# A recurrent kernel of 128 steps: biases loaded as single rows and spread by products with ones, x of steps 2 and 3 loaded later, sums and turns of the first steps rearranged

## The chip, the cores and the metric

The kernel runs on one core of one Trainium2 chip. The metric is device time in microseconds (us) from launch to end. Before the change the median of three runs is 1335.53 us (1335.13 to 1337.05).

## The reference

A gated recurrent unit runs over x (64 sequences, 128 steps, width 512) from the state h0 = cond_1024 (64 x 512), and its output is added to x. All is float32. Cut to what matters:

```python
def step(h, inp):
    x_t, prop = inp
    comb = jnp.concatenate([x_t, h], axis=-1)
    z = jax.nn.sigmoid(comb @ Wz + bz)
    r = jax.nn.sigmoid(comb @ Wr + br)
    comb2 = jnp.concatenate([x_t, r * h], axis=-1)
    h_cand = jnp.tanh(comb2 @ Wh + bh)
    h_new = (1.0 - z) * h + z * h_cand
    h_next = jnp.where(prop, jnp.tanh(h_new @ Wp + bp), h_new)
    return (h_next, h_new)
# prop holds at every fourth step but the last; the result is x + all h_new
```

Wz, Wr, Wh are 1024 x 512: the upper 512 rows meet x_t, the lower 512 meet the state. Wp is 512 x 512; bz, br, bh, bp have 512 elements.

## The kernel before

**Tiling.** The 64 sequences and two halves (S = 2) of the 512 columns together fill the 128 partitions: partition s*64 + b holds sequence b and columns s*256 to s*256 + 255. N = 256, C = 2 blocks of 128 columns each. A product (`product`, `products`, L191 to L205) multiplies one of four pieces of 128 rows of a weight with a turned left side, one matmul per half s into its 64 partitions. The weights over x are in `wx`, those over the state in `wh[0..2]` (R, Z, H in this order) and `wp`.

**The order of the work** is written out by hand, one queue for each engine; the schedule is manual, and each engine works its instructions in the order of the program. A step t (loop at L674) goes: products of the state with wh R (L723), sigmoid (L740), r*h; products with wh Z (L751), meanwhile the turns of r*h (L755), sigmoid twice for z and 1 - z (L764, L765), `keep` = (1-z)*h (L766); products of the turned r*h with wh H (L796), tanh (L802), two operations of VectorE that make h (L803, L808), and the turn of h for the next step (L820, L822). Every fourth step has the products with Wp as well. GpSimd adds h to x in place (L901).

**Filling.** What depends on x alone is put between these products as units out of a queue: `fill(n)` (L417) issues the next n units; the last unit of a batch leaves a function that empties its PSUM tiles, which `read_out()` (L424) issues later. PLACES and TAIL (L637 to L645) say how many units go where. The results, with the biases, are gathered in `cp`; `seed(i, t)` (L409) copies them into the PSUM tile of gate i (`rc`, `zp`), so that the products of the state are added on top.

**Two ways to the x products.** Steps 0 to 3 use `plain(t)` (L428): 12 units of plain products into scratch tiles (`scratch_q`, `_r`, `_a`, `_x`); plain(0) and (2) use q and r, plain(1) and (3) use a and x. From step 4 on, four steps are taken together and their products are made with fewer multiplications out of sums of x and sums of weights, twice nested. Sums of the weights: `sum_outer` (into `tw`, VectorE, L318), `sum_inner(i, eng)` (three operations into `tt`, L328) and `sum_inner_1(i, eng)` (one in place, L333), on VectorE or GpSimd as called. Sums of x: `sum_raw12`, `sum_raw34`, `sum_raw4`, `sum_s12`, `sum_s34` on GpSimd. A batch of them is made by `batch` (L509); before the change, batches of the first group of four steps (g = 1) write scratch q, r, x in this order after a, later ones r, x, q (L557). `pair_left` and `pair_right` (L623, L629) add the results of group 1 on GpSimd with the biases.

**Turning.** `turn` (L212) transposes one block of 128 columns by 4 matmuls against the identity (recorded as L219) into the PSUM tile `turn_0` or `turn_1`, and one copy (L210) takes it out. `turn_x(t, eng)` (L243) turns x of steps 0 to 7 in this way, with ScalarE copying where no engine is named. Later x is turned by a transposing DMA (`words_x`, `planes_x`, `join_x`).

**The head.** Before the steps (L72 to L153) the loads are issued: SyncE's queue holds the first half of x of steps 0, 1, then the weights in the order of use; ScalarE's queue holds the other half of that x and half of wx R. GpSimd waits at L130 (`held`) until x has landed, and then issues h0 and six loads of 64 KB that spread the rows of br, bz, bh over 64 partitions each (`load_bias`, L119). x of steps 2, 3 stands on SyncE's queue between wh R and wh Z (L138). TensorE meanwhile runs products of zeros (`idle(n)`, L179), turns x of steps 0 and 1, and does plain(0) and plain(1) with the turn of h0 in between (L657 to L669).

Of the kernel before, what the change touches and what calls it, by code (L numbers as in the profile page):

```python
# [9 lines left out]
F32 = mybir.dt.float32  # L10
BF16 = mybir.dt.bfloat16
# [6 lines left out]
def kernel(  # L18
# [29 lines left out]
    nc = tc.nc  # L48
    B, T, D = x.shape
    H = h0.shape[1]  # L50
    P = 128
# [19 lines left out]

    zeros = one.tile([P, 2 * N], BF16, tag="cq", name="zeros")  # L72
    nc.vector.memset(zeros, 0.0)
    ident = const.tile([P, P], F32, name="ident")
    make_identity(nc, ident)
    ones = const.tile([1, B], F32, name="ones")
    nc.gpsimd.memset(ones, 1.0)
    ident16 = const.tile([P, P], BF16, name="ident16")
    nc.vector.tensor_copy(ident16, ident)


    wx = const.tile([P, K, 3, H], F32, name="wx")
# [3 lines left out]
    tw = {n: const.tile([P, S, S, 3, P], F32, name=f"tw_{n}") for n in (2, 3, 4)}  # L86
    tt = const.tile([P, 7, 3, S, 3, P // 2], F32, name="tt")
    gates_in = (Wr, Wz, Wh)
    def load_x(tile_, t0, n, j=0):
        for s in range(S):  # L90
            nc.sync.dma_start(
                out=tile_[s * B : (s + 1) * B, j : j + n, :], in_=x[:, t0 : t0 + n, ts(s, N)]
            )
# [25 lines left out]
    def load_bias(i, eng):  # L119
        for s in range(S):  # L120
            eng.dma_start(
                out=bias_in[s * B : (s + 1) * B, i, :],
                in_=(br, bz, bh, bp)[i][ts(s, N)]
                .rearrange("(o n) -> o n", o=1)
                .broadcast_to([B, N]),
            )


    held = const.tile([1, 1], F32, name="held")
    nc.gpsimd.tensor_copy(held, xr[0][0:1, 0, 0:1])  # L130
    for s in range(S):
        nc.gpsimd.dma_start(out=h_init[s * B : (s + 1) * B, :], in_=h0[:, ts(s, N)])
    for i in (R, Z, H_):
        load_bias(i, nc.gpsimd)
    for i in range(3):
        for k in (0, 2):
            load_w(wh[i], gates_in[i][D:, :], k, k + 2, nc.sync)
        if i == 0:  # L138
            load_x(xr[0], 2, 2, 2)

    dummy = const.tile([1, 1], F32, name="dummy")
# [29 lines left out]

    def cut(ps):
        return ps.rearrange("p (c n) -> p c n", c=C)

    bias0 = bias[:, 0, 0:3, :]
    bias_d = const.tile([P, 3, P], F32, name="bias_d")
# [2 lines left out]
    def idle(n):  # L179
        for i in range(n):  # L180
            s = i % S
            nc.tensor.matmul(
                (rc, zp)[i // S % 2][s * B : (s + 1) * B, :, :],
                lhsT=zeros[:, :B],
                rhs=zeros,
                start=True,
                stop=True,
            )
# [14 lines left out]
    def product(ps, lT, w, k, start=False):  # L203
        s0, c0 = divmod(k, C)
        products(ps, lT[:, c0, ts(s0, B)], lambda s: w[:, k, ts(s, N)], start)  # L205
# [24 lines left out]
    def new_T(tag, name):  # L230
        return two.tile([P, C, P], F32, tag=tag, name=name)
# [11 lines left out]
    def turn_x(t, eng=nc.scalar):  # L243
        g, i = divmod(t, Q4)
        new_xT(g)
        src = xr[g] if g < 2 else early[g]
        for c in range(C):
            turn(src[:, i, :], xT[g][:, i], c, f"xT_{t}", eng)
# [79 lines left out]
    def sum_inner(i, eng):  # L328
        eng.tensor_sub(tt[:, i - 1, 1], inner(i, 1, 1), inner(i, 0, 1))
        eng.tensor_add(tt[:, i - 1, 0], tt[:, i - 1, 1], inner(i, 0, 0))  # L330
        eng.tensor_sub(tt[:, i - 1, 2], inner(i, 1, 0), tt[:, i - 1, 0])
# [31 lines left out]
    def sum_s12(g):  # L363
        v = xT[g]
        o = sx[g, "o12"] = one.tile([P, 2, 2, P], F32, tag="o12", name=f"o12_{g}")
        nc.gpsimd.tensor_add(o[:, 0], v[:, 2:4, 0, :], v[:, 2:4, 1, :])
        nc.gpsimd.tensor_sub(o[:, 1], o[:, 0], v[:, 0:2, 0, :])
        s = sx[g, 56] = one.tile([P, 4, 2, B], F32, tag="s56", name=f"s56_{g}")
        four([s[:, n] for n in range(4)], o[:, :, 0], o[:, :, 1])
# [139 lines left out]
    def batch(n, ms):  # L509

        def region(ps, m):
            return ps[:, m].rearrange("p g u -> p (g u)")

        def unit(ps, m, j, e, start):
            g, i = ms[m]
            a, b = terms(i)[e]
            products(
                region(ps, m),
                lhs(g, a, j),
                lambda s: factor(b, j)[:, s],  # L520
                start and m == 0 and e == 0,
            )

        def units(ps, j, start):
            return [
                lambda m=m, e=e: unit(ps, m, j, e, start)
                for m, (_, i) in enumerate(ms)
                for e in range(len(terms(i)))
            ]

        def blocks():
            return MB[n].rearrange("p m b g (a u) -> p m b a g u", a=2)

        def end_1():
            MB[n] = mbp.tile([P, 2, 2, 3, P], F32, tag="mb", name=f"mb_{ms[0][0]}_{ms[0][1]}")
            for m, (g, i) in enumerate(ms):
                M[g, i] = MB[n][:, m]
            nm = len(ms)
            T2[n] = one.tile([P, 2, 3, P // 2], F32, tag="cx", name=f"cx_{ms[0][0]}_{ms[0][1]}")
            q1 = one.tile([P, 2, 3, P // 2], F32, tag="cq", name=f"cq_{ms[0][0]}_{ms[0][1]}")  # L540
            nc.scalar.copy(T2[n][:, :nm], x_ps[:, :nm])  # L541
            nc.scalar.copy(q1[:, :nm], q_ps[:, :nm])
            nc.vector.tensor_add(T2[n][:, :nm], r_ps[:, :nm], T2[n][:, :nm])  # L543
            nc.vector.tensor_add(blocks()[:, :nm, 0, 0], a_ps[:, :nm], q1[:, :nm])

        def end_2():
            q2 = one.tile([P, 2, 3, P // 2], F32, tag="cq", name=f"cq2_{ms[0][0]}_{ms[0][1]}")
            nm = len(ms)
            nc.scalar.copy(q2[:, :nm], q_ps[:, :nm])  # L549
            nc.vector.tensor_add(blocks()[:, :nm, 0, 1], r_ps[:, :nm], q2[:, :nm])  # L550
            nc.vector.tensor_add(blocks()[:, :nm, 1, 0], x_ps[:, :nm], q2[:, :nm])
            nc.vector.tensor_add(blocks()[:, :nm, 1, 1], q_ps[:, :nm], T2[n][:, :nm])  # L552

        free = units(a_ps, 2, True)
        one_ = [units(r_ps, 5, True), units(x_ps, 7, True), units(q_ps, 1, True)]

        one_ = sum(one_ if ms[0][0] >= FIRST else one_[2:] + one_[:2], [])  # L557
        two_ = units(x_ps, 4, False) + units(q_ps, 6, False) + units(r_ps, 3, False)
        seq = [(u, None) for u in free + one_ + two_]
        size = sum(len(terms(i)) for _, i in ms)  # L560
        for n_units, end in ((4 * size, end_1), (7 * size, end_2)):
            seq[n_units - 1] = (seq[n_units - 1][0], end)
        return seq
# [59 lines left out]
    def pair_left(a, p1, p2):  # L623
        nc.gpsimd.tensor_add(
            M[1, p2], M[1, p2], bias0.unsqueeze(1).to_broadcast([P, 2, 3, P])
        )
        add(c_block(1, a, 0), m_(1, p1), m_(1, p2))
# [17 lines left out]
    )  # L645


    idle(24)
    turn_x(0, nc.vector)
    idle(8)  # L650
    turn_x(1, nc.vector)
    idle(12)
    nc.gpsimd.tensor_sub(bias_d, bias[:, 1, 0:3, :], bias0)
    h = h_init
    hT = new_T("hT", "hT_init")
# [18 lines left out]
    for t in range(T):  # L674
# [48 lines left out]
        for k in ORDER:  # L723
            product(slots[R], hT, wh[R], k)
        if t < 2:
            turn_x((2, 6)[t])
        if t == 1:
            for i in (7, 4):
                sum_inner(i, nc.gpsimd)
                sum_inner_1(i, nc.gpsimd)  # L730
        read_out()
        if t == 2:
            pair_left(0, 1, 2)
        if u == 0 and pair >= 1 and odd - 2 < LAST:
            outer_u2(odd - 2)
        if t == 3:
            sum_s12(FIRST)
        rh = two.tile([P, N], F32, tag="rh", name=f"rh_{t}")
        for c in range(C):
            nc.scalar.activation(act_ps[c], slots[R][:, ts(c, P)], AF.Sigmoid)  # L740
# [9 lines left out]

        for k in ORDER[: 2 if thin else 3]:  # L751
            product(slots[Z], hT, wh[Z], k)
        rhT = new_T("rhT", f"rhT_{t}")
        for c in range(C):
            turn(rh, rhT, c, f"rhT_{t}", nc.vector)  # L755
# [9 lines left out]
        nc.scalar.activation(slots[Z], slots[Z], AF.Sigmoid, scale=-1.0)  # L765
        nc.vector.tensor_mul(keep, slots[Z], h)  # L766
        join(1)
        if t == 1:
            sum_inner(5, nc.vector)
            sum_inner_1(5, nc.vector)  # L770
        seed(Z, t + 1)
        if prop:
            nc.scalar.copy(cut(slot_p), bias[:, :, 3, :])
# [40 lines left out]
            planes_x(3)  # L814
        read_out()
        fill(places[0] if thin else 5 if places[1] > 6 else 4)
        h = h_new
        if not last:
            hT = new_T("hT", f"hT_{t}")
            turn(h, hT, 0, f"hT_{t}", nc.vector)  # L820
            fill(places[1] if thin else 1 if places[1] > 6 else 2)
            turn(h, hT, 1, f"hT_{t}", nc.scalar)  # L822
        fill(places[2] if thin else places[1] - 6)
        if t == 0:
            sum_outer_1()
            for i in (1, 2, 3):
# [11 lines left out]
                turn(h, hT, c, f"hpT_{t}", (nc.vector, nc.scalar)[c])  # L838
            fill(behind[1] if thin else 2)
        if t == 0:  # L840
            turn_x(4)
            turn_x(5)
            sum_raw12(1)
        elif t == 1:
            turn_x(7)
            sum_raw34(1)
        elif t == 2:
            pair_right(0, 1, 10)
        elif t == 3:
            pair_left(1, 8, 9)  # L850
            pair_right(1, 8, 11)
# [35 lines left out]
                    outer_c12(odd)  # L887
        if u == 7 and pair >= -1 and (even + 2) * Q4 < T:
            sum_raw12(even + 2)
            if pair >= 0:  # L890
                sum_s12(even + 2)
        if pair >= 0:
            if u in (1, 2):
                for n in range(2):
# [74 lines left out]
```

## Time and profile before

| | before |
|---|---|
| median of 3 runs | 1335.53 us |
| lowest, highest | 1335.13, 1337.05 us |
| time of the profiled execution | 1334.71 us |
| span of the profiled execution, first to last instruction | 1332.9 us |
| granted TensorE clock, mean | 0.999 |
| TensorE busy | 1322.6 us (99%) |
| GpSimd busy | 932.5 us (70%) |
| VectorE busy | 706.6 us (53%) |
| ScalarE busy | 635.4 us (48%) |
| bytes moved by DMA | 77.79 MB, mean 58 GB/s |

All times within the profile count from the first instruction. PE is TensorE, PEld its weight loads, DVE is VectorE, ACT is ScalarE, POOL is GpSimd, SP is SyncE; a q behind a name is the queue's sequencer, which issues DMAs. A row of the timeline gives start and duration in us, engine, line, operation, output <- input, and in brackets the idle time of that engine before it and what ended it. A row of the waits gives the total, the number of times and the longest. A row of the chain of waits gives start, duration and what. A call of a float32 matmul shows as two rows in the records, so that a unit (two halves) has four; one turn has four rows. The recorded ends of matmuls are modelled and overlap the next one; starts are exact.

### The profile page before, as it was taken

The page shows a single profiled execution, that of the slowest core. Times are in us where ns is not written, and L with a number is a line of the kernel's source. Part 1 is how long each engine was busy: PE and PEld are TensorE (multiplying, and loading weights), DVE is VectorE, ACT ScalarE, POOL GpSimd, SP SyncE. Part 2 cuts the span into 40 slices and gives each one's busy share as a digit, 9 for nine tenths or more (in the row PEclk, how much of TensorE's full clock was granted, in tenths as well). Part 3 has the DMA queues.
Part 4 walks back from the last instruction along what each step waited for, and adds up shares of the span by engine and source line. Part 5 has one row for each costly group of instructions (what it writes and reads, how often), then busy time and mean ns, then how long its engine had stood idle before and what let it go on. Part 6 is the DMA issues. An engine that isn't in the chain of part 4 may idle for free.

```text
span 1332.9 us, 37646 instructions
## 1 busy us (share of the span) xinstructions
PE 1322.6 (99%) x15336; PEld 1115.6 (84%) x15336; DVE 706.6 (53%) x1874; ACT 635.4 (48%) x1860; POOL 932.5 (70%) x1135
## 2 busy tenths in 40 slices
PE   9999999999999999999999999999999999999998
PEld 5788888888888888888888888888888888888765
DVE  3555555555555555555555555555555555555444
ACT  1454455454544544545445454445545444554433
POOL 5687876777777768776787767786777687767400
PEclk9999999999999999999999999999999999999999
DMA  9222233121221222313112221222212222131300
GB/s 293 45 49 49 49 65 64 33 65 39 59 65 33 65 51 47 65 40 81 42 40 58 64 65 33 56 43 65 65 33 65 49 50 65 33 76 38 98 24 17
DMA packets 119277, 77.79 MB, mean 58 GB/s; under 512 B 65984, under 2 KB 114240, under 8 KB 119104
## 3 DMA queue, kind: packets, MB, share of 16 engines
q1 hardware_dynamic: 118352, 74.14, 24.1%
q8 instruction: 121, 1.98, 0.6%
q10 hardware_dynamic: 496, 0.72, 0.2%
q0 software_dynamic: 256, 0.52, 0.1%
q14 instruction: 52, 0.43, 0.1%
HBM read 42.86 MB, written 16.78 MB: 45 GB/s over the span
## 4 chain that ended last, share of the span: by engine, by line
PE 96%; DMA 2%; DVE 1%; POOL 1%; ACT 0%; issue 0%; SPq 0%; DVEq 0%; ACTq 0%; POOLq 0%
PE rc L194 33%; PE zp L194 20%; PE scratch_q L194 11%; PE scratch_r L194 10%; PE scratch_x L194 10%; PE scratch_a L194 6%; PE turn L219 5%; DMA wh<-in_L_cond_Wz_dram 1%; DMA wx<-in_L_cond_Wz_dram 1%; POOL cp L582 0%; POOL mb L630 0%; ACT xT L283 0%; SPq L96 0%; DVE wx L334 0%; DVE tt L330 0%
## 5 line engine op out<-in xcount | busy, mean ns | idle before, releaser
L194 PE MATMUL rc<-wh,rhT 128*64 128x256 f32 x2048 | 246.1, 379 | 0.0
L582 POOL TENSOR_TENSOR cp<-mb,mb 128x768 f32<-128x768 f32 x74 | 134.5, 1817 | 102.4 <-ACT rc L411 54.4
L194 PE MATMUL zp<-wh,hT 128*64 128x256 f32 x1536 | 204.5, 379 | 0.0
L194 PEld LDWEIGHTS rc<-wh,rhT 128*64 128x64 f32 x2048 | 168.9, 137 | 39.9
L194 PE MATMUL rc<-wh,hT 128*64 128x256 f32 x1536 | 186.3, 383 | 0.3
L901 POOL TENSOR_TENSOR xr<-xr,h 128x256 f32<-128x256 f32 x127 | 92.7, 730 | 105.2 <-DVE h L808 105.2
L194 PEld LDWEIGHTS rc<-wh,hT 128*64 128x64 f32 x1536 | 121.6, 137 | 36.2 <-issue 9.8
L582 POOL TENSOR_TENSOR cp<-mb 128x768 f32<-128x768 f32 x46 | 83.6, 1816 | 95.1 <-ACT rc L411 93.7
L194 PEld LDWEIGHTS zp<-wh,hT 128*64 128x64 f32 x1536 | 119.3, 137 | 24.8
L210 DVE COPY rhT<-turn 128x256 uint16<-128x256 uint16 x256 | 97.5, 420 | 79.9 <-PE turn L219 78.8
L803 DVE TENSOR_TENSOR turn<-turn,z 128x128 f32<-128x128 f32 x256 | 75.4, 294 | 120.9 <-ACT turn L802 119.3
L740 ACT ACTIVATE turn<-rc 128x128 f32<-128x128 f32 x256 | 55.3, 260 | 167.3 <-issue 111.6
L210 ACT COPY hT<-turn 128x256 uint16<-128x256 uint16 x127 | 47.3, 373 | 168.6 <-DVE hT L210 130.4
L582 POOL TENSOR_TENSOR mb<-mb,mb 128x768 f32<-128x768 f32 x58 | 105.4, 1817 | 9.5 <-DVE mb L552 9.5
L411 ACT COPY rc<-cp 128x256 f32<-128x256 f32 x256 | 96.4, 376 | 25.9 <-DVE cp L436 14.4
L550 DVE TENSOR_TENSOR mb<-scratch_r,cq 128x384 f32<-128x384 f32 (+1 forms) x105 | 58.4, 556 | 93.2 <-ACT cq L549 93.2
L802 ACT ACTIVATE turn<-rc 128x128 f32<-128x128 f32 x256 | 55.2, 260 | 105.0 <-PE rc L194 103.9
L543 DVE TENSOR_TENSOR cx<-scratch_r,cx 128x384 f32<-128x384 f32 (+1 forms) x105 | 58.3, 556 | 86.2 <-ACT cx L541 86.2
L764 ACT ACTIVATE z<-zp 128x256 f32<-128x256 f32 x128 | 49.2, 384 | 96.2 <-PE zp L194 96.2
L283 ACT COPY xT<-xv 128x512 uint16<-128x512 uint16 x120 | 91.3, 764 | 0.0
L808 DVE TENSOR_TENSOR h<-turn,keep 128x128 f32<-128x128 f32 x254 | 74.0, 291 | 15.2
L219 PEld LDWEIGHTS <-h 128*64 128x64 bf16 x1016 | 68.3, 110 | 14.3 <-DVE h L808 7.9
(163 smaller groups left out, 3026.8 us busy)
## 6 DMA issues: line engine op xcount, KB each, us to landing
xr<-in_x_dram SPq DMA_DIRECT2D x62, 256.0 KB, 4.0
out_dram<-xr SPq DMA_DIRECT2D x62, 256.0 KB, 3.3
xs<-in_x_dram SPq DMA_DIRECT2D x56, 256.0 KB, 4.3
wx<-in_L_cond_Wz_dram SPq DMA_DIRECT2D x2, 512.0 KB, 8.0
wx<-in_L_cond_Wh_dram SPq DMA_DIRECT2D x2, 512.0 KB, 11.4
wh<-in_L_cond_Wr_dram SPq DMA_DIRECT2D x2, 512.0 KB, 13.4
wh<-in_L_cond_Wz_dram SPq DMA_DIRECT2D x2, 512.0 KB, 11.8
wh<-in_L_cond_Wh_dram SPq DMA_DIRECT2D x2, 512.0 KB, 10.9
```

Of the source, the lines that this page charges most:

```text
L194: nc.tensor.matmul(ps[s * B : (s + 1) * B], lhsT=lhs, rhs=rhs(s), start=start, stop=True, skip_group_check=True,)
L210: (eng.copy if eng is nc.scalar else eng.tensor_copy)(dst, src)
L219: nc.tensor.transpose(pt[s * B : (s + 1) * B, w, :], words.rearrange("p (n w) -> p w n", w=2)[:, w, :], ident16,)
L283: nc.scalar.copy(xT[g][:, i].bitcast(U16).rearrange("p c (n w) -> p w c n", w=2), xv[g][:, i])
L411: nc.scalar.copy(cut(slots[i]), G[t][:, :, i, :])
L543: nc.vector.tensor_add(T2[n][:, :nm], r_ps[:, :nm], T2[n][:, :nm])
L550: nc.vector.tensor_add(blocks()[:, :nm, 0, 1], r_ps[:, :nm], q2[:, :nm])
L582: nc.gpsimd.tensor_add(dst, a, b)
L740: nc.scalar.activation(act_ps[c], slots[R][:, ts(c, P)], AF.Sigmoid)
L803: nc.vector.tensor_mul(pc, pc, z[:, ts(c, P)])
L808: nc.vector.tensor_add(h_new[:, ts(c, P)], pc, keep[:, ts(c, P)])
L901: nc.gpsimd.tensor_add(xr[g][:, j, :], xr[g][:, j, :], h_new)
```

## The change

1. The loads of br, bh and bz become three loads of one row of 512 elements (2 KB) each. They stand at the head of ScalarE's queue, ahead of its half of x, and land in partition 0 of `tt`, which has no other use yet. The function `spread` multiplies a column of 64 ones with these rows, one matmul per half s, into the scratch tiles x (R and H together) and a (Z); ScalarE copies them out to `bias_in`. bp is loaded as before.
2. `held` waits for the first part of wx R, no longer for x; h0 is issued behind it.
3. x of steps 2, 3 goes behind wh Z on SyncE's queue.
4. Idle products: 24, 8 and 12 become 16, 2 and none.
5. turn_x(2) goes from behind the R products of step 0 to behind three of the four Z products; turn_x(4) from the end of step 0 to between two groups of three units; turn_x(7), with `sum_raw34(1)`, from the end of step 1 to ahead of the turn of h.
6. The sums of the weights: 5 goes from VectorE to GpSimd, in the place of 4, ahead of 7; 4 goes to step 2, on GpSimd.
7. `sum_s12(FIRST)` goes from step 3 to the end of step 2, ahead of `pair_right(0, 1, 10)`, which goes behind it and behind `sum_raw12(2)`.
8. Batch (1, 2) writes its scratch tiles in the order r, x, q.

The diff, without the moved declarations of tiles:

```diff
+    bias_row = tt.rearrange("p a b c d e -> p (a b c d e)")[0:1, : 3 * H].rearrange(
+        "p (i n) -> p i n", i=3
+    )
+    for i, b in enumerate((br, bh, bz)):
+        nc.scalar.dma_start(out=bias_row[:, i, :], in_=b.rearrange("(o n) -> o n", o=1))
     ident = const.tile([P, P], F32, name="ident")
...
-    nc.gpsimd.tensor_copy(held, xr[0][0:1, 0, 0:1])
+    nc.gpsimd.tensor_copy(held, wx[0:1, 1, R, 0:1])
     for s in range(S):
         nc.gpsimd.dma_start(out=h_init[s * B : (s + 1) * B, :], in_=h0[:, ts(s, N)])
-    for i in (R, Z, H_):
-        load_bias(i, nc.gpsimd)
     for i in range(3):
         for k in (0, 2):
             load_w(wh[i], gates_in[i][D:, :], k, k + 2, nc.sync)
-        if i == 0:
+        if i == Z:
             load_x(xr[0], 2, 2, 2)
...
+    def spread(bank, rows, which):
+
+        bank = bank.rearrange("p (i n) -> p i n", i=2)
+        n = len(which)
+        for s in range(S):
+            nc.tensor.matmul(
+                bank[s * B : (s + 1) * B, 0:n, :],
+                lhsT=ones,
+                rhs=bias_row[:, rows, ts(s, N)],
+                start=True,
+                stop=True,
+            )
+        for j, i in enumerate(which):
+            nc.scalar.copy(bias_in[:, i, :], bank[:, j, :])
...
-        one_ = sum(one_ if ms[0][0] >= FIRST else one_[2:] + one_[:2], [])
+        one_ = sum(one_[2:] + one_[:2] if n in ((1, 0), (1, 1)) else one_, [])
...
-    idle(24)
+    idle(16)
     turn_x(0, nc.vector)
-    idle(8)
+    idle(2)
+    spread(scratch[3], slice(0, 2), (R, H_))
     turn_x(1, nc.vector)
-    idle(12)
+    spread(scratch[2], slice(2, 3), (Z,))
...
         if t < 2:
-            turn_x((2, 6)[t])
+            if t:
+                turn_x(6)
         if t == 1:
-            for i in (7, 4):
+            for i in (5, 7):
                 sum_inner(i, nc.gpsimd)
                 sum_inner_1(i, nc.gpsimd)
         read_out()
         if t == 2:
             pair_left(0, 1, 2)
+            sum_inner(4, nc.gpsimd)
+            sum_inner_1(4, nc.gpsimd)
...
-        if t == 3:
-            sum_s12(FIRST)
...
         for k in ORDER[: 2 if thin else 3]:
             product(slots[Z], hT, wh[Z], k)
+        if t == 0:
+            turn_x(2)
...
-        if t == 1:
-            sum_inner(5, nc.vector)
-            sum_inner_1(5, nc.vector)
         seed(Z, t + 1)
...
         fill(places[0] if thin else 5 if places[1] > 6 else 4)
+        if t == 1:
+            turn_x(7)
+            sum_raw34(1)
         h = h_new
...
-        fill(places[2] if thin else places[1] - 6)
+        if t == 0:
+            fill(3)
+            turn_x(4)
+            fill(3)
+        else:
+            fill(places[2] if thin else places[1] - 6)
...
         if t == 0:
-            turn_x(4)
             turn_x(5)
             sum_raw12(1)
-        elif t == 1:
-            turn_x(7)
-            sum_raw34(1)
-        elif t == 2:
-            pair_right(0, 1, 10)
...
             sum_raw12(even + 2)
-            if pair >= 0:
-                sum_s12(even + 2)
+            sum_s12(even + 2)
+        if t == 2:
+            pair_right(0, 1, 10)
```

More of the change, by code (lines that the diff above doesn't have):

```diff
@@ L73 @@
     nc.vector.memset(zeros, 0.0)
+    wx = const.tile([P, K, 3, H], F32, name="wx")
+    wh = [const.tile([P, K, H], F32, name=f"wh_{i}") for i in range(3)]
+    wp = const.tile([P, K, H], F32, name="wp")
+    tw = {n: const.tile([P, S, S, 3, P], F32, name=f"tw_{n}") for n in (2, 3, 4)}
+    tt = const.tile([P, 7, 3, S, 3, P // 2], F32, name="tt")
+    gates_in = (Wr, Wz, Wh)
+    bias_row = tt.rearrange("p a b c d e -> p (a b c d e)")[0:1, : 3 * H].rearrange(
[3 more added lines that the diff above has]
+        nc.scalar.dma_start(out=bias_row[:, i, :], in_=b.rearrange("(o n) -> o n", o=1))
     ident = const.tile([P, P], F32, name="ident")
@@ L79 @@
     nc.vector.tensor_copy(ident16, ident)
-    wx = const.tile([P, K, 3, H], F32, name="wx")
-    wh = [const.tile([P, K, H], F32, name=f"wh_{i}") for i in range(3)]
-    wp = const.tile([P, K, H], F32, name="wp")
-    tw = {n: const.tile([P, S, S, 3, P], F32, name=f"tw_{n}") for n in (2, 3, 4)}
-    tt = const.tile([P, 7, 3, S, 3, P // 2], F32, name="tt")
-    gates_in = (Wr, Wz, Wh)
     def load_x(tile_, t0, n, j=0):
```

## The prediction

> **What bounds the kernel now.** First the page, part 1: TensorE is busy for 1322.6 of 1332.9 us. All the rest of this text is therefore about the 10 us in which it is not, and about the start. The waits of TensorE say where they are; the view covers the whole span and has only these rows.
>
> ```profile
> PE turn L219 <- DVE h L808: 1.6, 2, 1.4
> PE rc L182 <- DVE zeros L73: 1.2, 1, 1.2
> PE zp L194 <- DMA wh<-in_L_cond_Wz_dram: 0.7, 1, 0.7
> PE scratch_q L194 <- DVE mb L552: 0.5, 1, 0.5
> PE turn L219 <- ACT hT L210: 0.4, 1, 0.4
> PE turn L219 <- ACT xT L210: 0.4, 1, 0.4
> PE scratch_r L194 <- POOL s L344: 0.2, 1, 0.2
> ```
>
> Each wait occurs once, and the chain of waits puts all in the first 77 us: up to 23.4 us it is made of DMA, then of matmuls, and around step 1 of VectorE:
>
> ```profile
> 12.17 11.19 DMA wh<-in_L_cond_Wz_dram
> ...
> 44.03 0.48 DVE tt L329
> ...
> 45.80 1.25 DVE tt L331
> 47.05 1.28 DVE wx L334
> 48.33 0.47 DVE cx L543
> 48.80 0.47 DVE mb L544
> 49.26 0.22 DVE turn L803
> ```
>
> The reader is to see that four sums of weights (tt, wx) stand ahead of the addition that makes the hidden state. From 77 us to the tail the engine has next to no gaps, so whatever the head saves comes off the end, one for one.
>
> The waits are understated, since the recorded end of a matmul is modelled. I price them by starts in the timeline, at the pace of its dense stretches: 8 rows of 192 columns take 0.65 us, 16 of 256 columns 1.73, 8 transposes 0.22.
>
> ```profile
> 22.07 0.65 PE L194 MATMUL zp<-wh,hT_init 128*64 128x256 f32 x4
> 23.41 1.08 PE L194 MATMUL zp<-wh,hT_init 128*64 128x256 f32 x8 [0.69 <-DMA wh<-in_L_cond_Wz_dram]
> 37.52 0.39 PE L219 MATMUL turn<-ident,xr 128*64 128x128 bf16 x8
> 38.27 0.58 PE L219 MATMUL turn<-ident,xr 128*64 128x128 bf16 x8 [0.36 <-ACT xT L210]
> 47.68 0.82 PE L194 MATMUL scratch_q<-tt,s12r 128*64 128x192 f32 x8
> 49.85 0.31 PE L219 MATMUL turn<-ident,h 128*64 128x128 bf16 x4 [1.35 <-DVE h L808]
> ```
>
> True gaps: 0.17 before and 0.91 inside the first zp product (four rows last 0.43: 22.07 to 22.50, next 23.41); 0.69 at turn_x(4), turn_x(5) (37.52, next product 38.66, where 0.45 would do); 1.52 before hT (48.33 to 49.85); 0.53 at turn_x(7); 0.74 at scratch_q (66.65 to 67.39); 0.38 at scratch_r (75.90 to 76.28). That is 4.9 us in all, and the first real product (L194) starts only at 9.37.
>
> **The start.** Idle products run from 1.20 at 0.427 us per pair, and at 0.216 from 7.42; the timeline shows the step:
>
> ```profile
> 6.75 0.62 PE L182 MATMUL rc<-zeros 128*64 128x512 bf16 x2
> 7.17 0.40 PE L182 MATMUL zp<-zeros 128*64 128x512 bf16 x2
> 7.42 0.38 PE L182 MATMUL rc<-zeros 128*64 128x512 bf16 x2
> 7.63 0.38 PE L182 MATMUL zp<-zeros 128*64 128x512 bf16 x2
> ```
>
> So the clock doubled at about 7.3 us, after 6.1 us of unbroken matmuls. In the change idle(16) ends at 1.20 + 16 x 0.213 = 4.6. turn_x(0) then waits for the half of x that ScalarE's queue loads, now behind three rows of biases. The issue of so small a load is not in the trace; larger ones took 0.37 to 0.76 us, so three cost between nothing and 2.3. I take 1.3, near the lowest row. The half is issued at 2.05 instead of 0.75, lands 2.9 to 3.5 later by the two rows for x, say at 5.3, and turn_x(0) starts at 5.4 after a pause of 0.8. At the slow clock there follow turn_x 0.43, two idle products 0.43, the first spread, turn_x 0.43 and the second spread. No float32 product of 512 columns or of one row is in the trace. Bounds for the first spread: 0.22 us (the pair of bf16 rows of that width) and 1.73 (two pairs of 256 columns take 0.43 each, doubled for width and again for the clock); I take the upper pace, as these are float32, and half for the second. Sum 3.88 us slow, 1.94 fast. If the clock needs its 6.1 us of work, it changes at 7.3 + 0.8 = 8.1: 2.7 us are done, 1.18 remain and take 0.59. First product at 8.7, against 9.37.
>
> [...]
>
> **The wait for Wz.** Ahead of wh Z the change drops 384 KB of spread biases (six loads of 64 KB on GpSimd's queue) and 256 KB of x. DMA is full at 315 to 343 GB/s there (windows 5 to 20 us), so 0.66 MB are worth 1.9 us: the second half lands at 23.37 - 1.9 = 21.45. TensorE gets to zp at 8.7 + 12.53 (9.37 to 21.90 before) - 0.22 (turn_x(2) is now behind it) = 21.0, and needs that half 0.43 later, 21.45: both agree. Three parts of zp end at 22.3. x of steps 2, 3 lands 0.26 MB later, 22.2: just in time. But turn_x(2) now stands directly ahead of the turns of rh, which use the same turn tiles, and must wait for ScalarE's copies. The row for two such turns in a row is 37.52 to 38.66, 1.14 us instead of 0.45; so 22.3 + 1.14 + 0.43 = 23.87 for the end of zp, against 24.98. **Gain 1.1.** The table load on ScalarE (1.28 us) slides to about 4.8, ahead of the three bias copies (0.38 each), which hide behind the first products (1.73 until scratch_a is written). GpSimd's six issues of biases (3.1 us) went into idle time. h0 now waits for wx instead of x: issued near 6.5, landing 6.2 later (row), 12.7 to 13.5, wanted at 8.7 + 6.9 = 15.6; if wx is as late as 7.9, as before, it is 14.9, still covered. wh H (27.3 before) comes earlier and is wanted at 29.
>
> **Steps 0 to 3.** Three units (1.3 us) between turn_x(4) and turn_x(5) cover ScalarE's two copies (0.65): **0.69**. In step 1 VectorE loses 0.55 + 1.24 + 1.25 + 1.36 of sums. Late next are ScalarE's cx, cq (46.45 to 47.3) and then tanh; h's first half would be there at 48.4 (cx 46.95, two sums at 0.47 pace, product and sum 0.5). turn_x(7) now fills 0.22 from 48.33, and hT waits for its copy: by the same row 0.75 after its start, 49.08. Two units later, the second half is turned, and step 2 begins at 49.95 instead of 51.50. **Gain 1.55**, both waits in it. GpSimd gets sums 5 in place of 4, the same eight sums from 41.8 to 51.2 as before, less contended; then s34r (1.8 us), done by about 51.2 when the queue starts 1.8 us earlier, which TensorE wants at 56.3 - 3.3 = 53.0. Sums 4 (4 to 5 us) fall into its idle 9.1 us before L630. In step 2 batch (1,2) writes scratch_r first: L550 leaves it at 66.4, so no wait at 66.65, but then hT waits for h at 67.93 instead of being turned at 68.41: **0.44** of 0.74. In step 3 s is long done: **0.38**. What is late next is pair_right: raw12 1.8 and s12 3.4 run ahead of it from 64.4, it ends at 73.4 and not 71.1, and ScalarE's seed (72.13) waits about 1.7 us for it. The seed and cq queue in front of z at 75.46; both need 0.8 after 73.8: hidden with about 0.9 to spare, one for one beyond it.
>
> **Sum.** 1.1 + 0.69 + 1.55 + 0.44 + 0.38 = 4.2 us. Own time of the profiled execution 1334.71 (span 1332.9 plus 1.8 around it) gives 1330.5; the median of the runs lies 0.8 above that execution, so 1335.5 - 4.2 = **1331.3**.
>
> **Rivals.** (a) *The clock comes late.* For: nothing in the trace shows that work before and after a pause adds up. Against: the pause is short beside 6.1 us. If the count starts anew at 5.4, the clock changes at 11.5: the preparation ends at 9.28, 2.2 us of products run at half pace and lose 1.1, an effective start at 10.4, and zp ends at 25.6: the gain of 1.1 turns into a loss of 0.6. Total 2.5, time 1333.0. (b) *GpSimd takes the bound* in steps 2 and 3: each us that pair_right is later than 0.9 after my reckoning is one us; contended sums took up to 1.77 instead of 1.0, which over four sums 4 is 3 us, partly in its idle time. Loss about 1, time 1332.3. (c) *Nothing arrives*: a transfer or GpSimd's chain holds step 4 where it was; against it, the transposed x is joined 3.3 us after landing (50.9, 54.3) and everything else follows TensorE. 1335.5. (d) *Slower*: the slow clock holds on, one mechanism. Every 2 us of slow products cost 1; the whole gain of 4.2 is used up and 2.7 more is lost when the change comes at 8.1 + 2 x 6.9 = 21.9 us, which gives 1338.2; from there on it decides. For it speaks only the pause, against it the unbroken work after 5.4.
>
> **How the numbers follow.** Forecast 0.55 (own range 1330.3 to 1332.4: with spread and loads at their low ends the products start a us earlier, but Wz and x of step 2 still land at 21.45 and 22.2, so I allow 1.0 for an earlier landing at most; with the loads at 2.3 us x lands at 6.4, the clock changes at 9.1, the products start at 9.75, and 1.05 is lost), (a) 0.22, (b) 0.10, (c) 0.07, (d) 0.06. About 0.2% (2.7 us, below 1332.9) is what a measurement can tell from no change. Faster: the forecast, (b) and half of (a), 0.76. Same: half of (a) and (c), 0.18. Slower: (d), 0.06. The range takes in (a) and (b): 1330.3 to 1333.6.
>
> **What would show it.** Right: first L194 product near 8.7; pairs of 0.216 us from about 8.1; no wait for Wz; no VectorE row tt or wx (L329 to L334) between 40 and 50 but the sums of step 0; step 2 starting 3.3 earlier; new small waits of turn on ScalarE's xT at steps 0 and 1. Wrong: pairs at 0.43 us among the products of scratch_q; x's second half landing after 6; a wait of z or of rc on L582 in step 3.

## The result, and the profile after

The changed kernel is slower: 1338.59 us (median of 19 runs, 1336.58 to 1340.05) against 1335.72 (1335.06 to 1337.48). The ratio is 1.0020, with a 95% interval of 1.0014 to 1.0026. The profiled execution took 1338.57 us, its span is 1336.8. The two profiled executions lie 3.9 us apart and the medians 2.9, since the one before the change (1334.71) was quicker than each of the 19 runs. The forecast was 1331.3 and faster.

The waits of TensorE in the changed kernel (engine, line, what it waited for, total, times, longest):

```profile
PE turn L239 <- DMA xr<-in_x_dram: 4.4, 1, 4.4
...
PE turn L239 <- DVE h L829: 0.6, 3, 0.2
PE turn L239 <- ACT xT L230: 0.4, 1, 0.4
PE scratch_r L214 <- DVE mb L570: 0.2, 1, 0.2
```

The wait for Wz is gone, that of hT on VectorE is down from 1.6 to 0.6, and scratch_q no longer waits. In their place stands one new wait of 4.4 us, for x. The timeline of the head shows where it comes from (start, duration, engine, line, operation):

```profile
2.11 0.71 ACTq L117 DMA_DIRECT2D xr<-in_x_dram  x1
...
9.02 0.64 PE L239 MATMUL turn<-ident,xr 128*64 128x128 bf16 x8 [4.41 <-DMA xr<-in_x_dram]
...
10.02 1.97 PE L185 MATMUL scratch_x<-tt,ones 1*64 1x512 f32 x4
...
12.49 1.12 PE L185 MATMUL scratch_a<-tt,ones 1*64 1x256 f32 x4
13.54 3.68 PE L214 MATMUL scratch_q<-wx,xT 128*64 128x256 f32 x16
```

ScalarE issued its half of x at 2.11, as forecast (2.05), but it landed 6.8 us later and not 3.2. The first product starts at 13.54 instead of 8.7, and 16 rows of it take 3.68 us against 1.89 before the change: about half pace. The table by stage gives the granted clock (column PEclk, after the five engines). The column does not show the slow stretch ahead of the first rise: it reads 1.00 from the start in every trace here, also where pairs of idle products take 0.43 us. The times given for the clock come from the traces' own records of its changes, and the pace of the products agrees with them.

```profile
4.30:7.70 3.40, 0.32 (x4) 0.00 (x0) 0.00 (x0) 0.69 (x2) 1.31 (x3) 1.00 1.06 321
7.70:17.90 10.20, 8.88 (x48) 3.98 (x50) 1.51 (x4) 1.02 (x3) 3.60 (x4) 0.50 1.05 356
17.90:26.30 8.40, 8.40 (x86) 5.54 (x84) 2.38 (x5) 1.06 (x3) 6.26 (x7) 1.00 1.09 264
```

The clock came up at 4.27, fell to one half at 7.69 in the pause, and came back at 17.93; 16 rows took 3.47 us by starts ahead of that and 1.72 behind it. Step by step the two traces, by the first R product of a step on the state, read so:

| start of step | before | after | difference |
|---|---|---|---|
| 0 | 19.95 | 26.33 | +6.38 |
| 1 | 38.66 | 43.91 | +5.25 |
| 2 | 51.50 | 55.49 | +3.99 |
| 3 | 69.62 | 73.35 | +3.73 |
| 4 | 86.71 | 90.45 | +3.74 |
| 127 | 1322.23 | 1326.25 | +4.02 |

The head loses 6.4 us: 4.17 until the first product and 2.2 over the 4.4 us of products at half clock. Steps 0 to 2 give 2.65 back; the forecast had about 3.5 behind the start of step 0 (4.2 less the 0.67 of the earlier first product). The 0.28 between steps 4 and 127 are not accounted for here. So most of what the steps were to bring came, and the head decided.

### The profile page after: what moved, and what is told of

Its sections match the earlier page's. It is cut to its first block, busy times and chain, and to the rows that moved or that the text cites. A ratio compares the mean times of both kernels' runs of the same rounds, so it can differ in the third digit from the quotient of the medians.

```text
span 1336.8 us, 37607 instructions
## 1 busy us (share of the span) xinstructions
PE 1324.6 (99%) x15318; PEld 1113.2 (83%) x15318; DVE 702.7 (53%) x1870; ACT 637.9 (48%) x1863; POOL 933.3 (70%) x1133
## 4 chain that ended last, share of the span: by engine, by line
PE 97%; DVE 1%; ACT 1%; DMA 1%; issue 0%; ACTq 0%; DVEq 0%
PE rc L214 33%; PE zp L214 20%; PE scratch_q L214 11%; PE scratch_r L214 11%; PE scratch_x L214 11%; PE scratch_a L214 6%; PE turn L239 5%; DMA xr<-in_x_dram 1%; ACT xw L230 0%; PE scratch_x L185 0%; DVE h L829 0%; DVE turn L824 0%; ACT xT L303 0%; ACTq L88 0%; DVE mb L570 0%
## 5 line engine op out<-in xcount | busy, mean ns | idle before, releaser
L570 DVE TENSOR_TENSOR mb<-scratch_r,cq 128x384 f32<-128x384 f32 (+1 forms) x105 | 58.4, 556 | 92.8 <-ACT cq L569 92.8
```

## The experiments

Two theories were set against each other. *Order of the queues*: the rows delay ScalarE's loads by 1.4 us, SyncE's loads reach the DMA engines first, and the later queue waits for their backlog. *Small loads*: three loads of 2 KB are slow or block their queue themselves. For the clock: *lost by the pause and by products over one row*, or *a matter of busy time alone*.

**rows_alone**: the kernel before, with three rows that nobody uses.

```diff
+    for i, b in enumerate((br, bh, bz)):
+        nc.scalar.dma_start(out=bias_row[:, i, :], in_=b.rearrange("(o n) -> o n", o=1))
```

> The kernel before with nothing but the three row loads added at the head of ScalarE's queue; nobody uses the rows. Theory (order of the queues): x's second half lands at about 9 instead of 4.2, TensorE pauses from 6.3 to 9, first product at 11.7 to 14, time 1337 to 1339.5. Rival (the rows cost only their issue, 1.4 us): x lands at 5.6, inside the idle products, and the time stays within 0.3 us of the kernel before.

Measured: 1339.07 us (1337.97 to 1341.73), ratio 1.0032 (1.0019 to 1.0045). x is turned at 8.54, and the half of wx R behind it comes later still:

```profile
8.54 0.42 PE L224 MATMUL turn<-ident,xr 128*64 128x128 bf16 x8 [2.02 <-DMA xr<-in_x_dram]
...
14.00 1.30 PE L199 MATMUL scratch_q<-wx,xT 128*64 128x256 f32 x10 [2.23 <-DMA wx<-in_L_cond_Wr_dram]
```

The rows alone, without any of the rest, cost as much as the whole change. The traced execution is the fastest of the five. Its clock came up at 6.67 and did not fall through the waits of 2.02 and 2.23 us (0.22 us a pair from 8.76, 12 rows from 14.00 in 1.35 by starts), so its loss, 3.28 us at the start of step 127, is put down to the late landings alone. The other four took 1.1 to 3.8 us longer at a lower mean clock (0.997 and 0.998 against 0.999), so the same kernel also lost time to the clock; that these waits did it is the author's estimate, as none of the four was traced.

The shares of the queues between 3 and 6 us (q1 is SyncE's, q10 ScalarE's; packets, MB and share of 16 engines come from the view of DMA) show where x was held up. The kernel before, where the two had near even parts, but in turns (from 4 to 5 us 182 packets of ScalarE's queue and 3 of SyncE's, from 5 to 6 us 15 and 150):

```profile
q10 hardware_dynamic: 282, 0.53, 56.0%
q1 hardware_dynamic: 259, 0.41, 38.9%
```

The changed kernel, same stretch:

```profile
q1 hardware_dynamic: 443, 0.87, 94.9%
q10 hardware_dynamic: 1, 0.00, 0.0%
```

One packet of 444 went to ScalarE's queue in this stretch, although its x was issued from 2.11 to 2.82. In rows_alone it was 1 of 438.

**late_issue**: the kernel before, with ScalarE's first activation and table load ahead of its loads; no rows.

```diff
     new_xr(0)
+    dummy = const.tile([1, 1], F32, name="dummy")
+    nc.scalar.activation(dummy, ones[:, 0:1], AF.Sigmoid)
     for s in range(S):
...
-    dummy = const.tile([1, 1], F32, name="dummy")
-    nc.scalar.activation(dummy, ones[:, 0:1], AF.Sigmoid)
```

> The kernel before with one move: ScalarE loads its table and makes its first activation ahead of issuing its two loads instead of behind them. No rows are loaded. ScalarE's half of x is then issued near 2.2 us, as late as in the changed kernel. Theory (order of the queues): it lands near 8.5 to 9 and the half of wx R at 12.4 to 14, time 1338 to 1339.5 as with the unused rows (1339.07). Rival (the small loads themselves block the queue): x lands at 5.5 to 6, hidden behind the idle products, time within 0.5 us of the kernel before.

Measured: 1341.57 us, ratio 1.0042 (1.0029 to 1.0056). ScalarE issued x at 1.44 already, earlier than expected, and it landed at 6.7; the half of wx R went out at 3.73 and landed at 14.6, for 4.5 us of wait:

```profile
14.69 2.83 PE L194 MATMUL scratch_q<-wx,xT 128*64 128x256 f32 x12 [4.54 <-DMA wx<-in_L_cond_Wr_dram]
```

No small load is in this kernel, so small loads are not needed for the delay: x was issued 0.7 us later than before the change and landed 3.1 later, wx R 2.2 and 9.0. The theory of the small loads falls as the explanation. The expectation missed when x would be issued, and so that it landed at 6.7 and not 8.5.

**rows_behind**: the changed kernel, the rows behind x and wx R on ScalarE's queue.

```diff
-    for i, b in enumerate((br, bh, bz)):
-        nc.scalar.dma_start(out=bias_row[:, i, :], in_=b.rearrange("(o n) -> o n", o=1))
...
+    for i, b in enumerate((br, bh, bz)):
+        nc.scalar.dma_start(out=bias_row[:, i, :], in_=b.rearrange("(o n) -> o n", o=1))
     def load_bias(i, eng):
```

> The changed kernel with its three row loads moved behind x and wx R on ScalarE's queue; all else as changed. Theory (order of the queues: the rows let SyncE's queue reach the DMA engines first, and it then keeps them, so the half of x on ScalarE's queue waits): x lands near 4.3 as before the change, the pause of TensorE is gone, the first product starts at 7.9 to 8.7, zp ends near 23.9, time about 1331.6. Rival (fewer idle products: the clock is lost whatever the loads do, or the products with ones are what is late): the slow clock lasts beyond 12 us, first product after 11, time 1335 to 1338.

Measured: 1335.4 us (1333.57 to 1335.6), ratio 0.9995 (0.9985 to 1.0004); forecast 1331.6. The profiled execution, with 1333.68, is among its two fastest. The other eight lie at 1335.05 or above, with a mean clock of 0.997 against 0.998, so they lost more to the clock than the trace shows. x is in time (turned at 4.73), which confirms half of the theory; the median is 3 us below the changed kernel. But now the rows are the late ones, and the clock goes up at 5.43, down at 8.85 and up at 12.26 (the first 16 rows of products take 3.08 us by starts):

```profile
7.32 1.07 PE L186 MATMUL scratch_x<-tt,ones 1*64 1x512 f32 x4 [1.64 <-DMA tt<-in_L_cond_bh_dram]
```

**long_idle**: the changed kernel with 44 idle products for 16.

```diff
-    idle(16)
+    idle(44)
```

> The changed kernel with idle(44) for idle(16), so that TensorE works until x lands at 9.0. Theory (two costs, the late x and the clock lost in the pause): the clock is fast when x lands, the preparation takes 1.9 us, the first product starts at 11, waits at its second part for the half of wx R that landed at 12.4, and the head is 3 to 4 us shorter: time about 1335. Rival (only the late landing costs, the clock does not): time within 1 us of the changed kernel, 1338.

Measured: 1335.97 us, ratio 1.0002 (0.9993 to 1.0011), 2.6 us below the changed kernel. x still is turned at 9.04, the preparation takes 2.5 us instead of 4.5 and the first product starts at 11.54. So of the head's 6.4 us some 2.3 (by the start of step 0, 24.04 against 26.33) to 2.6 (by the medians) or more are the clock and not the late landing. The clock did not hold: it fell at 12.09 and came back at 15.5, after a pause of only 0.9 us and two products over one row (the granted clock was 0.60 from 11.4 to 14.8 us and 0.90 from 14.8 to 18.2).

```profile
9.04 0.42 PE L239 MATMUL turn<-ident,xr 128*64 128x128 bf16 x8 [0.92 <-DMA xr<-in_x_dram]
```

In the trace of rows_alone twice that pause (2.02 and 2.23 us), without such products, left the clock up. So the pause is not the whole reason here, and the next run tries products over one row.

**one_row_idle**: the kernel before, its idle products over one row.

```diff
-                lhsT=zeros[:, :B],
-                rhs=zeros,
+                lhsT=zeros[0:1, :B],
+                rhs=zeros[0:1, :],
```

> The kernel before with its 44 idle products taken over one row of zeros instead of 128; as many instructions of the same length, same output. It measures whether products over one row keep the clock up, as the products with ones would have to. Theory (they count for little): the clock does not double before real products have run, that is not before 12 us; products of the preparation run at half pace up to then, and the time is 1.5 to 4 us above the kernel before. Rival (the clock counts busy time alone): the clock doubles between 4.6 and 8 us and the time is the same.

Measured: 1338.76 us (1337.91 to 1339.08), ratio 1.0019 (1.0010 to 1.0028). The engine is as busy as before from 1.2 us on, but a pair still takes 0.43 us at 11:

```profile
11.15 0.63 PE L182 MATMUL rc<-zeros 1*64 1x512 bf16 x2
11.57 0.63 PE L182 MATMUL zp<-zeros 1*64 1x512 bf16 x2
12.13 3.36 PE L194 MATMUL scratch_q<-wx,xT 128*64 128x256 f32 x16
```

The clock doubles at 15.04, 2.9 us after the first product with weights (12.13), which runs over 128 rows, against 7.21 before. From 1.20 to 12.13 products over one row, with two turns among them, did not raise the clock. The products with ones also run over one row; that they count as little is argued from this, not shown by itself.

**rows_behind_idle**: rows_behind with more idle products until the rows land.

```diff
-    idle(2)
+    idle(20)
```

> As rows_behind (rows moved behind x and wx R on ScalarE's queue), with idle(20) for idle(2), so that TensorE works on zeros until the rows land at 7.3. Theory (both causes mended): the clock stays up, first product near 9 at full pace, state products of step 0 at 19.7 to 20.2 against 21.53 in rows_behind, 1.4 to 1.8 us faster than rows_behind, time about 1332.5 to 1333.5 where rows_behind has its lower times. Rival (the two products with ones alone still drop the clock): no gain, state products of step 0 at 21.5 or later.

Measured: 1332.82 us (1332.01 to 1337.85), ratio 0.9980 (0.9971 to 0.9990), 2.6 below the median of rows_behind. In the trace the clock came up at 6.75 and stayed, through a wait of 0.8 us and the two products with ones (16 rows from 11.08 in 1.78 by starts): these do not drop it every time. One run of nine, 1337.85 at a mean clock of 0.997, lost it. The traced execution (1333.81) is no faster than that of rows_behind (1333.68); the gain is over the other eight runs there. The landings were missed: the rows landed at 9.1, not 7.3, and the first product started at 11.08, not 9.

**rows_sync** and **one_queue** take the rows off the queue whose large loads they share. In the first they stand on SyncE's queue behind its wx R, in the second ScalarE's two large loads go to SyncE's; both have idle(14) for idle(2).

```diff
-    for i, b in enumerate((br, bh, bz)):
-        nc.scalar.dma_start(out=bias_row[:, i, :], in_=b.rearrange("(o n) -> o n", o=1))
...
+        if i == R:
+            for r, b in enumerate((br, bh, bz)):
+                nc.sync.dma_start(out=bias_row[:, r, :], in_=b.rearrange("(o n) -> o n", o=1))
```

> The changed kernel with the three rows on SyncE's queue, directly behind its half of wx R, and idle(14) for idle(2). ScalarE's queue is as in the kernel before: half of x, half of wx R. Theory (who reaches the DMA engines late on the second queue waits for the backlog of the first): x lands near 4.3, wx R by 8, the rows, no longer behind on the second queue, by 7, first product at 8.5 to 9.5, clock kept, state products of step 0 near 20 instead of 21.7 in rows_behind_idle; time 1330.5 to 1332. Rival (small loads are slow wherever they stand): rows at 9 or later and the time of rows_behind_idle, 1332.8.

Measured: 1331.84 us (1331.74 to 1332.18), ratio 0.9971 (0.9960 to 0.9983). x is turned at 4.62, the rows are there when the idle products end, and the first product starts at 9.24 at full pace, 16 rows in 1.78 by starts:

```profile
7.31 1.07 PE L186 MATMUL scratch_x<-tt,ones 1*64 1x512 f32 x4
...
9.24 1.95 PE L215 MATMUL scratch_q<-wx,xT 128*64 128x256 f32 x16
```

```diff
-        (nc.sync, nc.scalar)[s].dma_start(
+        nc.sync.dma_start(
...
-                wx[:, :, i, :], gates_in[i], k, k + 2, nc.scalar if (i, k) == (R, 2) else nc.sync
+                wx[:, :, i, :], gates_in[i], k, k + 2, nc.sync
```

> The changed kernel with the rows still at the head of ScalarE's queue, but with both of that queue's large loads (half of x, half of wx R) moved to SyncE's queue, ahead of the other weights, and idle(14) for idle(2). Theory: the rows land by 4 and hold up nothing, x lands by 5, wx R near 8, first product at 8 to 9, time 1330.5 to 1332. Rival (one queue alone fills the DMA engines worse): wx R after 9, time above 1333.

Measured: 1332.05 us, ratio 0.9980 (0.9969 to 0.9991), but in two groups: eight runs lie at 1331.45 to 1332.43, two at 1337.5. The profiled execution is one of the two: x was turned at 5.86, after a pause of 1.0 us, and the clock did not come up before 17.12, with 3.68 us for the first 16 rows of products. TensorE worked at half pace from 5.86 to 17.12, which is 5.6 us lost by estimate, about the 5.5 between the two groups of runs. None of the eight was traced; that they had the same pause and kept the clock is likely, not shown.

**steps_alone**: the kernel before with the edits of steps 0 to 3 alone (turn_x(4) and (7), sums 4, 5, s12, pair_right, order in batch (1,2)).

```diff
-        one_ = sum(one_ if ms[0][0] >= FIRST else one_[2:] + one_[:2], [])
+        one_ = sum(one_[2:] + one_[:2] if n in ((1, 0), (1, 1)) else one_, [])
...
-            for i in (7, 4):
+            for i in (5, 7):
...
+        if t == 1:
+            turn_x(7)
+            sum_raw34(1)
         h = h_new
```

> The kernel before with only the rearrangement of steps 0 to 3: turns of x 4 and 7, sums 4, 5 and s12, pair_right, the order r, x, q in batch (1,2). The head, the loads and turn_x(2) are as before. From the trace of the changed kernel (step 0 to 1 without its two head terms 0.7, step 1 to 2 1.26, step 2 to 3 0.26, step 3 nothing): 2.2 us faster than before, 1333.4. Prediction on record: 0.69 + 1.55 + 0.44 + 0.38 = 3.1, 1332.5. Rival (the gains are given back later): no change.

Measured: 1332.88 us, ratio 0.9983 (0.9973 to 0.9992), 2.7 below before (forecast 2.2 and 3.1). This half of the change is a gain, and it stays in rows_sync and one_queue.

**steps_x7_late** and **steps_x7_after** are steps_alone with turn_x(7) moved to step 2, ahead of read_out or behind it.

```diff
-        if t == 1:
-            turn_x(7)
-            sum_raw34(1)
...
-        if t < 2:
-            turn_x((2, 6)[t])
+        if t < 3:
+            turn_x((2, 6, 7)[t])
+        if t == 2:
+            sum_raw34(1)
```

> As steps_alone (the rearranged steps with the head of the kernel before), with turn_x(7) and its sums behind the R products of step 2 instead of ahead of the turn of h in step 1. Theory (turn_x(7) writes the turn tiles that VectorE still reads for h, so it cannot fill the wait and lengthens it): the gap of 0.24 + 0.42 + 0.12 before step 2 shrinks to about 0.1, 0.5 to 0.8 us faster than steps_alone, 1332.2 against 1332.9. Rival (the copies of ScalarE are late whatever the place): no change against steps_alone.

Measured: 1334.33 us, ratio 0.9988 (0.9980 to 0.9997): 1.4 above steps_alone, a miss. Step 1 did become 0.7 shorter, but a wait of 1.2 us came up in step 2, because ScalarE copies x7 ahead of cq:

```profile
51.62 0.65 ACT L210 COPY xT<-turn 128x256 uint16<-128x256 uint16 x2 [1.56 <-PE turn L219]
52.16 0.50 ACT L549 COPY cq<-scratch_q 128x384 f32<-128x384 f32 x1
...
54.23 1.03 PE L194 MATMUL scratch_q<-wx,xT 128*64 128x192 f32 x10 [1.23 <-DVE mb L552]
```

```diff
         if t == 2:
+            turn_x(7)
+            sum_raw34(1)
             pair_left(0, 1, 2)
```

> As steps_x7_late, with turn_x(7) behind read_out in step 2 instead of ahead of it, so that ScalarE's copy of cq, for which VectorE's L550 to L552 wait, comes first. Theory (the 1.4 us that appeared at scratch_q in steps_x7_late are this order on ScalarE's queue): that wait is gone, step 2 still begins 0.7 earlier than in steps_alone, time 0.5 to 0.7 below steps_alone: about 1332.3. Rival (the wait at scratch_q comes from the shorter step 1 itself): it stays above 1 us, time 1334.

Measured: 1332.67 us, ratio 0.9977 (0.9968 to 0.9986). The wait at scratch_q is gone, step 1 is 0.71 shorter than in steps_alone and step 2 0.24 longer. Of the 0.47 the medians show 0.2, or 0.4 when each is set against the kernel before of its own set of runs; the intervals overlap, so no gain in time is shown.

**rows_sync_x7**: rows_sync with that same move.

> rows_sync with turn_x(7) and its sums behind read_out in step 2, as in steps_x7_after: both mends in one kernel. If the two parts add up: 1331.84 less the 0.47 that steps 1 and 2 of steps_x7_after were shorter than in steps_alone (step 1 0.71 shorter, step 2 0.24 longer), 1331.4, and the fastest kernel of this study. If the head sets the end of step 1 another way: 1331.8, no gain over rows_sync.

Measured: 1332.25 us (1331.89 to 1334.49), ratio 0.9976 (0.9965 to 0.9986). Its step 4 starts 0.37 earlier than that of rows_sync, but the median is 0.4 above; the two were timed in different sets, and their intervals overlap. In its trace TensorE also waited 0.5 us each for x and for the rows, which rows_sync did not. No gain is shown, and rows_sync remains the fastest kernel here with 0.29% below the kernel before.

## Why the prediction was wrong

- **x's late half, the step that failed.** The prediction let a load that is issued 1.3 us later land 1.3 us later, "2.9 to 3.5 later by the two rows for x". The issue was right (2.11), the landing 8.9 instead of 5.3. The rows for x came from a head in which nothing of SyncE's stood ahead of ScalarE's x: its queue moved 134 packets from 2 to 3 us, SyncE's 38. The profile before held a hint: of two halves of wx R issued at 1.51 and 1.56, ScalarE's landed in 4.1 us and SyncE's in 6.3. The queues took turns there (182 packets to 3 from 4 to 5 us, 15 to 150 from 5 to 6), and the half issued later landed some 2.2 us after the other. rows_alone and late_issue show this cause without the rest of the change. The forecast gave no price to ScalarE's half of wx R either; it landed at 12.4, in time only because the first product did not start before 13.54, and in rows_alone it cost 2.23 us by itself.
- **The clock, the second step that failed.** The forecast let work before and after the pause add up to 6.1 us and so set the change at 8.1; it counted the products with ones as work. Measured: up at 4.27 after 3.1 us of work, down at 7.69, up at 17.93. Rival (d), the slow clock that holds on, is what happened in kind. That its 1338.2 is near the 1338.59 is luck: it put the whole loss on the clock, with x in time and a change at 21.9, while 4.17 of the measured 6.4 us are the late first product. one_row_idle, long_idle and one_queue put the price of the clock at 2.6 to 5.5 us.
- **Products with ones.** The pace was right: two slow ones took 1.9 and 1.05, two fast ones about 1.0 and 0.6 (rows_sync), against the forecast's 1.73 and 0.86 for slow ones.
- **Wz and x of steps 2, 3.** Right in kind: no wait for either, in the changed kernel, which comes to step 0 late, and in rows_sync, which comes to it at 19.88, about as early as before. The turns of x2 ahead of rh cost 0.69, the row they were priced by. Step 0 was 1.13 shorter than before: zp's gaps of 1.08 and the 0.69 at turn_x(4) and (5) are gone, and the 0.69 at x2 is new, which makes 1.08.
- **Step 1.** 1.26 measured for 1.55. turn_x(7) did not fill the wait: its two halves start at 53.83 and 54.36, each right after VectorE's sum for h that reads the same turn tile.

```profile
54.36 0.31 PE L239 MATMUL turn<-ident,xr 128*64 128x128 bf16 x4 [0.22 <-DVE h L829]
```

- **Step 2.** 0.26 for 0.44.
- **Step 3.** Nothing for 0.38. The gap stays 0.39 and only changes its name: from s of GpSimd to mb L570 of VectorE, which had ended at the same time before. pair_right ended 1.2 us after ScalarE wanted it, and z did not wait, as forecast.
- **GpSimd** did not take the bound (rival b): s34r was ready at 57.2 for a use at 60.5.

The sum of the steps was forecast at 3.1 and came to 2.7 in steps_alone. With the head as in rows_sync, which has all edits but the place of the rows and the number of idle products, 1331.84 was measured beside a forecast of 1331.3. The mechanism of the gain in the steps was right, and two edits at the start undid it. The nearness of the number is partly luck: in the traces step 127 of rows_sync starts 2.8 us earlier than before the change (1319.46 against 1322.23), while the medians differ by 3.9, and no trace shows the other 1.1.

## What to carry to other kernels

A load's landing time cannot be read off a row of the same load in another order of issue: here 0.7 to 2.2 us later in issue became 3.1 to 9.0 later in landing. Before putting anything ahead of a large load on a second queue, look at what the first queue will have issued by then; in rows_sync the small loads did no harm behind the first large ones of the first queue (x was turned at 4.62, and the rows were there for their first use at 7.31). Idle products that are to keep the clock up should span the longest wait that can occur, and run over more than one row: over one row pairs still took 0.43 us at 11 in one_row_idle, over 128 rows 0.22 from 7.42 on in the kernel before. In one_queue, with a wait of 1 us in the trace, two runs of ten took 5 us longer, and rows_alone kept the clock through waits of 2 us in its trace but had a lower mean clock in its other four runs. A single trace does not tell whether a wait is safe. A gap with two producers that end together is not won by moving one of them (step 3: 0.38 before, 0.39 after).

## What the runs showed of the hardware

- **Two queues.** From 3 to 6 us of the changed kernel SyncE's queue moved 443 of 444 packets, with x issued on ScalarE's from 2.11 to 2.82. From 6 to 7 us the two moved 127 and 97, from 9 to 10 us 94 and 101. In late_issue, where x was issued at 1.44, ScalarE's moved 144 of 521 from 3 to 6 us, while SyncE's had work too. So the parts were near even in these stretches after 6 us, and one-sided from 3 to 6 us in the changed kernel. No trace shows whether ScalarE's packets already stood before the engines then, so what held them back stays open; that loads are served about in the order of their issue, whatever the queue, was not tried apart.
- **The spacing of the clock's changes.** The changes in the changed kernel lie 3.41 and 10.24 us apart, in rows_behind 3.41 and 3.41, in long_idle, where it came up at 5.26, 6.83 and 3.41: one, two or three times 3.41. The first rise came anywhere from 4.08 (rows_sync_x7) to 7.21 (before), with idle products from 1.20 in both. one_row_idle, busy from 1.2 us and slow until 15.04, shows that busy time alone did not raise it there. How many rows suffice was not tried.
